# Masks of an attention stack between VectorE and GpSimd: ten steps of 32 in place of eleven, placed otherwise, and the output transposition ordered behind the mask of its own step

## The chip, the cores and the metric

The kernel runs on one core of one Trainium2 chip. The metric is the time of one execution on the device in microseconds (us), the median of several runs. Engines are named as the profile names them: PE is TensorE, DVE is VectorE, ACT is ScalarE, POOL is GpSimd, SP is the engine whose queue issues the DMAs. L557 is line 557 of the kernel.

## The reference

Sixteen sequences of 1024 tokens with 128 features go through three transformer layers with a shared adjacency mask and then through one graph attention layer. Cut to what matters:

```python
# layers 0 to 2 (8 heads of 16)
scores = einsum('bnhd,bmhd->bhnm', Q, K) / sqrt(16)
scores = where(adj == 0, -inf, scores)
attn_out = einsum('bhnm,bmhd->bnhd', softmax(scores), V)
x = layer_norm(x + attn_out @ Wo + bo)
x = layer_norm(x + relu(x @ W1 + b1) @ W2 + b2)
# layer 3: one head, scores s_i + s_j through a leaky relu, same mask, softmax, out + x, layer norm
```

## The kernel before, in words

**Passes and steps.** The work is cut into 48 passes. A pass is one sequence in one of the layers 0 to 2; four sequences go through the three layers side by side, so 12 passes make a round and there are four rounds. A pass has 32 steps: two groups of four heads, in each two halves of 512 queries, in each eight tiles of 128 keys. The line `order` in the main loop sets this sequence; n, held in `now[0]`, counts steps over the whole kernel.

**One step** (`score_step`, L537). Two score tiles of 128x1024 are made, each by two matmuls (L545) into a PSUM tile of the tag s, of which there are three (`slot`, L135). The first tile is called pp 0, the second pp 1. Each has to be masked and exponentiated, and there are two ways. On the POOL way ACT takes the exponential straight out of PSUM (L553) and POOL multiplies it by a mask of zeros and ones (L554). On the DVE way DVE adds a mask of zeros and large negative numbers while it reads PSUM (L557), and ACT takes the exponential in place (L569). pp 1 always goes the DVE way. pp 0 goes the POOL way, except in the steps that `BOTH_ON_DVE` (L41) names by their number within the pass, where both tiles go the DVE way. The PSUM tile is free again once L553 or L557 has read it.

**The sum over keys** (`av_step`, L571) follows four steps later (`AHEAD`, L40): eight matmuls (L574) add e times V into the one PSUM bank acc. After the eight key tiles of a half, at steps 3, 11, 19 and 27 of a pass, `finish` (L577) transposes acc on DVE (L585) into the tile tt, takes the reciprocals of the sums (L588, DVE) and lets POOL multiply (L589). The next half writes acc again from the following step on, so it has to wait for the transposition.

**Everything else** is a list of tasks, put into steps by the table `AT` (L34) and taken by `piece` (L871): projections of the next pass at steps 5 to 19 (`proj_tasks`, L457; ACT writes hi in L472 or L476, DVE writes the remainder lo in L473 or L477), the output projection of the pass before at 13 and 15, its first feed-forward matrix at 23 to 29 and its second at 31 and, of the pass before that, at 3. These matmuls (L383) use one PSUM bank, t. The sums and the norm's statistics are on DVE (L420, L413, L415), the norm itself on POOL (L433 to L435 and L441; all eight tiles at step 6 or so, four tiles each after steps 14 and 16), scale and shift on POOL (L511, L515, L632). DVE transposes x for the next layer and for the feed-forward (L357), and SP moves the result through memory (L361, L375). SP also copies hi and lo into the stacked form that the scores read (`stack`, L523). The graph attention of a finished sequence (`last_tasks`, L701) runs as further tasks during passes 10 to 14 of a round, in eight units of 128 queries (the loop of L826), with its edge masks on DVE (L774) and its norm and scaling on POOL (L798).

**What sets the order.** In the main loop PE, ACT and SP take their instructions in the order in which the program names them (`manual_schedule`, L957). DVE and POOL are ordered by a scheduler from priorities, before the kernel runs; on the chip they too run one instruction after the other in that order. Two tools correct the scheduler. `soon` (L333) raises the priority of an instruction by 120 places. `tc.issue_after(i)` puts an instruction behind instruction i on its engine. `behind["dve"]` holds the last mask addition that was named, `low` the lo instruction of each step that has one. L557 itself is put behind the lo of two steps earlier, where there is one.

Of the kernel before, what the change touches and what calls it, by code (L numbers as in the profile page):

```python
# [37 lines left out]
STACK_AT = 24  # L38
AT_END = {3: (12, 21, 22, 24, 25, 26, 27, 28, 30, 31), 2: (8, 9, 13, 14, 15, 16, 17, 18, 20, 21)}
AHEAD = 4  # L40
BOTH_ON_DVE = (2, 6, 7, 8, 17, 21, 23, 25, 26, 29, 30)  # L41
TILES = {"w": 8, "x": LANES + 1, "last": 2}
BLOCKED = -57344.0

# [75 lines left out]
def fast_path(ctx: ExitStack, tc: tile.TileContext, a: dict, out: bass.AP, flag):  # L120
# [24 lines left out]
    head, tail = [True], [False]  # L145
# [187 lines left out]
    def soon():  # L333

        return nullcontext() if head[0] else tc.high_priority(offset=SOON)
# [185 lines left out]
    behind, low = {}, {}  # L521
# [15 lines left out]
    def score_step(step):  # L537
# [3 lines left out]
        for pp in range(2):  # L541
# [6 lines left out]
            psv = ps.rearrange("p (r q) -> p r q", q=512)  # L548
            both = now[0] % (4 * NT) in BOTH_ON_DVE
            on_pool = pp == 0 and not both  # L550
# [26 lines left out]
    def finish(g, qh, acc):  # L577

        def run():
            if g == 0 and qh == 0:  # L580
                state["A"] = work.tile([P, 2, 16, G, HD], F32, tag="A", name="A", bufs=1)
                state["recs"] = work.tile([P, G, 2, 16], F32, tag="recs", name="recs", bufs=2)
            tt = work.tile([P, 16, SLOT], F32, tag="tt", name="tt", bufs=1)
            with soon(), tc.issue_after(low[now[0] - 2]) if now[0] - 2 in low else nullcontext():
                nc.vector.transpose(tt.rearrange("p a b -> p (a b)"), acc)  # L585
            rec = state["recs"][:, g, qh, :]
            with soon():
                nc.vector.reciprocal(rec, tt[:, :, HD])  # L588
                nc.gpsimd.tensor_mul(state["A"][:, qh, :, g, :], tt[:, :, :HD],  # L589
                                     rec[:, :, None].to_broadcast([P, 16, HD]))  # L590
        return run
# [246 lines left out]
    now = [0]  # L838
# [404 lines left out]
```

## Time and profile before

| what | value |
|---|---|
| median of 3 runs | 3936.28 us (3936.0 to 3938.77) |
| profiled execution, its own time | 3936.96 us |
| its span, first to last instruction | 3935.1 us |
| PE / DVE / ACT / POOL busy | 3742.7 / 3512.1 / 3289.2 / 3386.4 us |
| mask additions on DVE (L557) | 2064 of 1209 ns |
| mask multiplications on POOL (L554) | 1008 of 2026 ns |
| exponentials on ACT, from PSUM (L553) and in place (L569) | 1008 of 1024 ns, 2064 of 1061 ns |
| output transpositions on DVE (L585) | 192 of 706 ns |
| a pass without graph attention, such as the one from 469.65 to 540.58 us | 70.9 us |
| passes 10 to 15 of the first round (graph attention in them) | 74.0, 98.9, 91.3, 92.5, 95.3, 81.0 us |

How to read it: a busy time is a sum over the whole span, so a share says little about any one stage. PE's ends are modelled, so a busy PE is not PE at its peak. The start of a pass is the start of its first L545 matmul; the lengths of passes in the table are differences of such starts, and the start of each step follows by counting four L545 matmuls a step.

### The profile page before, as it was taken

The numbers are of one execution on the slowest core, as the hardware profiler recorded it, in microseconds if no ns is written. First come the engines' busy times: TensorE is split into PE (matmuls) and PEld (weight loads), VectorE is DVE, ScalarE is ACT, GpSimd is POOL, SyncE is SP. The second block draws the span as 40 slices with busy tenths as digits, with TensorE's granted clock in tenths as the row PEclk, the third lists the DMA queues.
The fourth block names the chain that finished last, engine by engine and source line by source line (L and its number), as shares of the span: only waits on it lengthen the run. The fifth ranks groups of instructions, "written<-read, shape, count | busy, mean of one in ns | idle before, by whom it ended". The sixth has DMA issues, their size and how long they took to land.

```text
span 3935.1 us, 109752 instructions
## 1 busy us (share of the span) xinstructions
PE 3742.7 (95%) x44385; PEld 1519.1 (39%) x44385; DVE 3512.1 (89%) x5908; ACT 3289.2 (84%) x3797; POOL 3386.4 (86%) x2923
## 2 busy tenths in 40 slices
PE   7999999999989999999998999999999999999987
PEld 2333333344434333334444433333444433333346
DVE  6999999989989999998998999998898999999876
ACT  7989999977877999997777899998776799999850
POOL 4889999978888999997888999998887899999784
PEclk8999999999999999999999999999999999999998
DMA  5423424322223423332322324333231324324200
GB/s 137 117 69 96 99 71 109 86 66 70 71 66 92 101 71 104 86 86 69 79 71 77 90 68 103 90 79 98 69 88 51 85 68 100 95 73 110 56 8 21
DMA packets 245889, 319.30 MB, mean 81 GB/s; under 512 B 51073, under 2 KB 174209, under 8 KB 245377
## 3 DMA queue, kind: packets, MB, share of 16 engines
q1 hardware_dynamic: 243840, 311.52, 31.3%
q8 instruction: 354, 5.80, 0.6%
q14 instruction: 159, 1.29, 0.1%
q10 hardware_dynamic: 1536, 0.68, 0.1%
HBM read 58.53 MB, written 51.38 MB: 28 GB/s over the span
## 4 chain that ended last, share of the span: by engine, by line
PE 50%; DVE 22%; ACT 11%; issue 6%; POOL 5%; DMA 3%; SPq 3%; DVEq 0%; ACTq 0%; POOLq 0%
PE acc L574 18%; DVE e L557 15%; PE t L383 15%; PE s L545 13%; ACT e L569 5%; ACT e L553 3%; POOL e L554 2%; PE s L769 2%; ACT hT L649 2%; PE s L383 1%; DMA x1T<-tr 1%; DVE st L413 1%; POOL x L441 1%; DVE xb L357 1%; DVE aT L603 1%
## 5 line engine op out<-in xcount | busy, mean ns | idle before, releaser
L557 DVE TENSOR_TENSOR e<-s,mask_add 128x1024 f32<-128x1024 f32 x2064 | 2417.5, 1209 | 136.7 <-PE s L545 99.2
L554 POOL TENSOR_TENSOR e<-e,mask 128x1024 f32<-128x1024 f32 x1008 | 2028.6, 2026 | 387.6 <-ACT e L553 373.8
L569 ACT ACTIVATE e<-e 128x1024 f32<-128x1024 f32 x2064 | 2144.6, 1061 | 176.9 <-DVE e L557 152.2
L574 PE MATMUL acc<-e,v 128*17 128x512 f32 x12288 | 1628.2, 602 | 12.7 <-POOL e L554 9.3
L545 PE MATMUL s<-Wq,Wk 64*128 64x512 f32 x6144 | 1228.6, 461 | 74.6 <-DVE e L557 32.0
L553 ACT ACTIVATE e<-s 128x1024 f32<-128x1024 f32 x1008 | 1031.9, 1024 | 294.1 <-PE s L545 279.5
L545 PEld LDWEIGHTS s<-Wq,Wk 64*128 64x128 f32 x6144 | 503.6, 185 | 1157.5 <-DVE e L557 464.3
L441 POOL TENSOR_SCALAR x<-x,mv 128x128 f32<-128x128 f32 x896 | 388.1, 448 | 19.5
L574 PEld LDWEIGHTS acc<-e,v 128*17 128x17 f32 x12288 | 205.7, 95 | 515.4 <-issue 428.3
L435 POOL TENSOR_TENSOR mv<-mv,half_neg 128x4 f32<-128x4 f32 (+1 forms) x179 | 213.9, 1195 | 14.1
L420 DVE TENSOR_TENSOR x<-t,x 128x512 f32<-128x512 f32 x191 | 131.9, 690 | 100.0 <-PE t L383 96.7
L413 DVE BATCH_NORM_STATS2 st<-x 128x6 f32<-128x128 f32 x896 | 204.6, 282 | 9.0
L774 DVE SCALAR_TENSOR_TENSOR ee<-s,mask 128x256 f32<-128x256 f32 x512 | 179.5, 412 | 32.4 <-PE s L769 32.4
L383 PE MATMUL t<-hd,ee 128*32 128x129 f32 x6656 | 205.7, 274 | 2.7 <-DVE x L420 2.7
L383 PE MATMUL t<-x1T,W 128*32 128x512 f32 x1520 | 199.3, 596 | 4.8 <-issue 2.4
L383 PEld LDWEIGHTS t<-W,hT 128*32 128x32 f32 x6080 | 169.2, 110 | 60.1 <-issue 48.7
L383 PEld LDWEIGHTS t<-hd,ee 128*32 128x32 f32 x6656 | 178.8, 109 | 16.4 <-DVE x L420 5.3
L383 PE MATMUL t<-W,hT 128*32 128x128 f32 x6080 | 183.6, 273 | 0.2
L585 DVE STREAM_TRANSPOSE tt<-acc 128x512 f32<-128x512 f32 x192 | 135.6, 706 | 33.4 <-PE acc L574 33.4
L649 ACT ACTIVATE hT<-t,b 128x512 f32<-128x512 f32 x190 | 130.6, 688 | 4.9 <-PE t L383 4.4
L515 POOL TENSOR_TENSOR x<-x,bo 128x1024 f32<-128x1024 f32 x48 | 114.6, 2388 | 9.2 <-DMA ai<-in_adj_dram 6.7
L589 POOL TENSOR_TENSOR A<-tt,recs 128x256 f32<-128x256 f32 x192 | 119.8, 624 | 0.2 <-DVE recs L588 0.2
(145 smaller groups left out, 2536.5 us busy)
## 6 DMA issues: line engine op xcount, KB each, us to landing
Wk<-hi SPq DMA_DIRECT2D x384, 128.0 KB
Wk<-lo SPq DMA_DIRECT2D x384, 128.0 KB
Wq<-hi SPq DMA_DIRECT2D x384, 128.0 KB
Wq<-lo SPq DMA_DIRECT2D x384, 128.0 KB
tr<-xb SPq DMA_DIRECT2D x656, 64.0 KB
x1T<-tr SPq DMA_DIRECT2D x90, 256.0 KB
xT<-tr SPq DMA_DIRECT2D x74, 256.0 KB
x<-in_x_dram SPq DMA_DIRECT2D x124, 64.0 KB
```

What stands on the lines that cost most here:

```text
L383: nc.tensor.matmul(dst[j:j + SLOT, :], cols, rhs, start=start, stop=stop)
L413: nc.vector.bn_stats(st[:, t, :], z[:, t, :])
L435: nc.gpsimd.tensor_tensor(v, v, half_neg[:, ts], OP.pow)
L441: nc.gpsimd.tensor_scalar(z[:, t, :], z[:, t, :], mv[:, t, 0:1], mv[:, t, 1:2], op0=OP.add, op1=OP.mult)
L545: nc.tensor.matmul(ps[:, r * 512:(r + 1) * 512], k[64 * r:64 * r + 64, kt * P:(kt + 1) * P], q[64 * r:64 * r + 64, q0:q0 + 512], start=Tru ...
L553: nc.scalar.activation(ev, psv, AF.Exp, scale=HD ** -0.5)
L554: behind["pool"] = nc.gpsimd.tensor_mul(ev, ev, m).ins
L557: behind["dve"] = nc.vector.tensor_add(ev, psv, m).ins
L569: nc.scalar.activation(ev, ev, AF.Exp, scale=HD ** -0.5)
L574: nc.tensor.matmul(acc[j * SLOT:j * SLOT + HD + 1, :], v_bufs[m % 2][:, kt, 2 * j + g, :], e[:, j, :], start=first, stop=last)
L649: nc.scalar.activation(s["h", f, h], ps, AF.Relu, bias=w["b1"][:, f:f + 1], scale=1.0)
L774: nc.vector.scalar_tensor_tensor(e[:, :, j * SLOT:(j + 1) * SLOT], ps.rearrange("p (k q) -> p k q", q=P)[:, :, j * SLOT:(j + 1) * SLOT], 1 ...
```

## The change

Two edits. The set of steps in which both tiles are masked on DVE has ten members in place of eleven, five of the ten are new places (3, 15, 24, 28, 31), and six old ones are gone (2, 6, 17, 21, 25, 29). And the transposition of acc (L585) is ordered behind the last mask addition that was named, which is that of its own step, in place of the lo of two steps earlier where there is one. The graph attention in eight units is in both kernels; the change does not touch it.

```diff
-BOTH_ON_DVE = (2, 6, 7, 8, 17, 21, 23, 25, 26, 29, 30)
+BOTH_ON_DVE = (3, 7, 8, 15, 23, 24, 26, 28, 30, 31)
...
             tt = work.tile([P, 16, SLOT], F32, tag="tt", name="tt", bufs=1)
-            with soon(), tc.issue_after(low[now[0] - 2]) if now[0] - 2 in low else nullcontext():
+            with soon(), tc.issue_after(behind["dve"]) if not tail[0] else nullcontext():
                 nc.vector.transpose(tt.rearrange("p a b -> p (a b)"), acc)
```

In the built programs PE's instructions stand in the same order before and after. On DVE and POOL the order differs. For a pass without graph attention, L557 and L554 written as the number of their step and the rest as their line, it is (STATS short for the statistics L413 and L415, NORM for L433 to L441):

```
DVE before   0 1 2 2 3 585 588 420 STATS 4 5 6 6 7 7 8 8 9 603 603 453 10 477 585 11 588 12 477 13 420 STATS
             14 15 420 STATS 16 17 17 357 477 18 19 585 588 20 477 21 21 357 22 23 23 24 357 25 25 26 26
             27 585 588 28 357 29 29 30 30 31 420 STATS
DVE after    0 1 2 3 3 585 588 420 STATS 4 5 6 7 7 8 8 9 603 603 453 10 477 11 585 588 12 477 13 420 STATS
             14 15 15 420 16 STATS 17 357 477 18 19 585 588 477 20 21 357 22 23 23 24 24 357 25 26 26
             27 585 588 28 28 357 29 30 30 31 31 420 STATS
POOL before  0 1 3 589 4 5 NORM8 9 10 11 589 12 13 14 NORM4 15 16 NORM4 18 19 589 20 22 632 24 632 27 589 28 511 515 31
POOL after   0 1 2 589 4 5 6 NORM8 9 10 11 589 12 13 14 NORM4 16 17 NORM4 18 19 589 20 21 22 632 632 25 27 589 511 29 515
```

## The prediction, made before the changed kernel ran

> **What bounds the kernel now.** I read the busy times first. No engine is idle enough to forget, so the question is who waits in a pass.
>
> ```profile
> PE 3742.7 (95%) x44385; PEld 1519.1 (39%) x44385; DVE 3512.1 (89%) x5908; ACT 3289.2 (84%) x3797; POOL 3386.4 (86%) x2923
> ```
>
> Then the busy times by stage, for one pass without graph attention (last line) and its parts: steps 0-3, 4-21, 22-28 and 29-31. Columns: stretch, its us, then busy us of PE, PEld, DVE, ACT, POOL.
>
> ```profile
> 469.65:478.32 8.67, 8.64 (x116) 3.67 (x112) 8.35 (x16) 7.71 (x8) 6.79 (x4) 1.00 0.64 161
> 478.32:517.48 39.16, 37.81 (x380) 12.97 (x376) 36.55 (x62) 36.48 (x41) 36.02 (x39) 1.00 0.17 42
> 517.48:532.59 15.11, 14.94 (x113) 4.12 (x109) 14.83 (x16) 14.89 (x18) 15.09 (x9) 1.00 0.49 123
> 532.59:540.58 7.99, 7.82 (x112) 3.49 (x108) 6.73 (x7) 7.78 (x9) 7.91 (x6) 1.00 0.70 162
> 469.65:540.58 70.93, 69.21 (x708) 24.25 (x704) 66.46 (x99) 66.86 (x74) 65.81 (x55) 1.00 0.36 87
> ```
>
> DVE, ACT and POOL all have 66 of 70.9 us, and POOL is already full from step 22 to the end. For PE I count from the timeline: an unhindered step (scores and sum) starts the next after 1.64 us; other matmuls add 0.86 or 0.87 in twelve steps and 1.75 in two. 32 x 1.64 + 12 x 0.865 + 2 x 1.75 = 66.4. So PE loses 4.5 us a pass. Where, PE's timeline shows: always ahead of the second score tile of a step, which needs a PSUM tile back.
>
> ```profile
> 492.85 0.50 PE L545 MATMUL s<-Wq,Wk 64*128 64x512 f32 x2
> 493.76 0.50 PE L545 MATMUL s<-Wq,Wk 64*128 64x512 f32 x2 [0.41 <-DVE e L557]
> ...
> 511.78 0.50 PE L545 MATMUL s<-Wq,Wk 64*128 64x512 f32 x2 [0.60 <-ACT e L553]
> ```
>
> By step the loss is 0.31 (step 3), 0.37 (9), 0.68 (11), 0.53 (13), 0.87 (19) and 1.6 together in 21, 22, 23, 25 and 29. At 9, 11 and 13 it is DVE that is late. DVE's timeline says why at 11: it stands idle at the transposition L585, which waits for PE's last sum, while the mask of step 11 queues behind it.
>
> ```profile
> 492.49 1.21 DVE L557 TENSOR_TENSOR e<-s,mask_add 128x1024 f32<-128x1024 f32 x1
> 493.62 0.74 DVE L477 SCALAR_TENSOR_TENSOR lo<-t,bqkv,hi 128x512 fp32r<-128x512 f32 x1
> 495.31 0.72 DVE L585 STREAM_TRANSPOSE tt<-acc 128x512 f32<-128x512 f32 x1 [0.95 <-PE acc L574]
> 495.95 1.18 DVE L557 TENSOR_TENSOR e<-s,mask_add 128x1024 f32<-128x1024 f32 x1
> ```
>
> POOL's timeline shows its only idle time in the pass: 1.80 ahead of the mask of step 3, 0.25 (step 4), 1.05 (9), 0.41 (10), 0.39 (14), each for an exponential of ACT.
>
> ```profile
> 477.19 2.03 POOL L554 TENSOR_TENSOR e<-e,mask 128x1024 f32<-128x1024 f32 x1 [1.80 <-ACT e L553]
> 491.08 2.02 POOL L554 TENSOR_TENSOR e<-e,mask 128x1024 f32<-128x1024 f32 x1 [1.05 <-ACT e L553]
> 493.51 4.01 POOL L554 TENSOR_TENSOR e<-e,mask 128x1024 f32<-128x1024 f32 x2 [0.41 <-ACT e L553]
> 502.45 2.03 POOL L554 TENSOR_TENSOR e<-e,mask 128x1024 f32<-128x1024 f32 x1 [0.39 <-ACT e L553]
> ```
>
> **What the Trainium skill says.** "Perfetto Trace Analysis", Identifying the Most-Contended Engine: a busy share measures Vector, Scalar and GpSimd fairly, PE's matmul share does not; hence my own count for PE (69.2 busy, 66.4 needed). The same page, Optimization Strategy, takes a gap that repeats as a sign of too few buffers; the gap ahead of the second score tile is one, with three s tiles. "PSUM — Partial Sum Buffer", Engine vs sequencer instructions: the queues of ScalarE, VectorE and GpSimdE are strictly first in, first out; the 0.95 us of L585 with a mask behind it agree. "GPSIMD Engine Reference", 3.1 Elementwise, has a two-input add take 1.96 times as long on GpSimd as on VectorE; here it is 2026 to 1209 ns, 1.68, and I use those.
>
> **The change part by part.** Sums are against the profiled execution, 3936.96 us (span 3935.1), 0.7 above the median of 3936.28.
>
> *Eleven to ten.* 48 masks leave DVE and go to POOL, one a pass. DVE loses 1.21 us a pass (66.46 to 65.25); POOL gains 2.03 (65.81 to 67.84); ACT has one L553 of 1024 ns for one L569 of 1061 ns, nothing. POOL becomes the fullest engine, and 67.8 a floor. DVE's relief pays only where DVE is last; POOL's load costs nothing only if it falls into POOL's idle 3.9 us.
>
> *Where it falls on POOL.* From the order: between the masks of steps 14 and 4 of the next pass POOL had 13 multiplications and the 1.80 us of idle time; now it has 14 and no wait for step 3. The idle time takes the 2.0 us. Between steps 4 and 13 it had eight (3, 4, 5, 9-13; 3 is replaced by 6) and still has eight, so the norms at 14 and 16 start as before. The order around 18 to 20 is the same too, 16 and 17 standing where 15 and 16 stood.
>
> *Steps 3 and 9 to 13 (PE).* Without the second mask of step 6 everything on DVE from there is 1.13 us earlier (the distance of two masks in the timeline): the wait of 0.37 at 9 goes, that at 11 shrinks to some 0.3. With L585 behind mask 11, that mask needs not wait for PE's sum: it starts at once, some 1.7 us earlier, so mask 12 and the wait at 13 (0.53) go. Step 3's wait halves, since ACT, not DVE, now frees that tile. Together 1.4 us.
>
> *Steps 15 to 22.* The mask of 17 (pp 0) is exchanged for that of 15, that of 21 for one of 24: DVE is where it was at 17 and ahead from 21. ACT gets to step 18 some 0.3 earlier; 0.4 of the 0.87 at step 19 goes. Steps 21 to 23 wait for ACT as before.
>
> *Steps 24 to 31.* The waits at 25 and 29 (0.28 + 0.44) go, as DVE is 1.1 ahead. That makes 2.5 us a pass for PE alone.
>
> *What is late next: POOL.* Follow it from the mask of step 4, for which it must wait for ACT (1.65 after the step's start, as now). Up to the mask of 18 there are 12 multiplications at 1.98 (start to start), eight norm tiles 5.86, two times four 6.94, one L589 0.58: 37.2, with 0.2 for the wait at 6. The sum over step 18 is due 0.7 into step 22. So steps 4 to 21 take at least 1.65 + 37.4 - 0.7 = 38.35, against 39.16. Steps 22 to 28: 19, 20, 21, 22, 25, one L589, two L632 of 2.36 make 15.2; now 15.11, so nothing is won. Steps 29 to 3: PE needs 15.9, and now takes 16.66. In all 69.45, a gain of 1.4 to 1.5 a pass, 1.4 taken.
>
> *The transposition alone.* At 3, 19 and 27 L585 already stood behind its step's mask; only step 11 changes. The wait that it adds: L585 and L588 stand behind a mask of 1.2 us, and PE's next sum (step 12) behind L585. Mask 11 ends as PE's last sum ends, so L585 ends some 0.3 before PE wants acc; without that cover it costs up to 0.9 a pass.
>
> *DMA.* No transfer is added. The copies that feed the next pass's scores are issued up to 534.94 and wanted at 540.58, and start from the L357 of step 22, which is not later.
>
> *Graph attention passes.* There PE is nearly never kept waiting (90.8 of 91.26 us busy in pass 12), so little is to be had: passes 12 to 14 -0.5 each; pass 11 +1, since POOL has one mask more ahead of step 27, whose sum had 0.9 us to spare. Pass 15 is the bad one: there POOL is behind, its masks of 15, 18, 19 and 20 end just as PE needs them, and one more (step 17) ahead of 18 costs up to 2.0, taken as 1.5. Passes 10, 22, 34, 46: -0.5 each.
>
> *Sum.* 25 plain passes (3-9, 16-21, 28-33, 40-45) x -1.4 = -35; passes 1 and 2 -2; the four -2; three rounds of passes 11-15 with (1 - 1.5 + 1.5) +3; pass 0 and the end after pass 46 nothing, as chains of DMA and PE set them (bounds -2 and +4). -36: 3901 in the profile's terms, 3900 as a median.
>
> **The rivals.** (a) *POOL does not pace* (0.20): what I count as POOL's chain has slack, and PE's 2.5 us come through: 25 x -2.5 and -5 elsewhere, 3868. For: ACT may come earlier as well. Against: POOL is full from step 22. (b) *No change* (0.14): the waits move from DVE to ACT and POOL, and a pass stays at 70.9; 3936, at most 8 either way. For: ACT's waits at 19 to 23 stay. (c) *Slower, through POOL* (0.20): POOL's idle 3.9 us stay because they wait for ACT, not for work. Then a pass needs 67.84 and what is left of them; from 3.1 us on it is slower than 70.93. With all 3.9 and 0.6 lost in turning from one engine to the other it is 72.3, 25 x 1.4 and three times 2 in pass 15: 3977. It shows as PE waiting at the sums of 18 to 25. Against: the idle time ahead of step 3 goes by the order alone. That the eight units do something is no case: they are in both kernels.
>
> **How the numbers follow.** The likeliest (0.46) is 3900, its own range 3884 to 3918. With (a) down to 3856 and (b) up to 3944 this holds 0.8; since (c) is open above, I take 3858 to 3956. About 0.2%, 8 us, is what can be told from no change. Faster by more: 0.46 + 0.20 + 0.02 = 0.68; within: 0.12; slower: 0.20.
>
> **What would show it.** Plain passes of 69 to 70 us; POOL at 98% in them; no wait of L585 for PE at step 11 beyond 0.3; PE's waits at 9 and 13 gone, new short ones at the sums of 18 to 25 for POOL. It is wrong if PE's waits for PSUM tiles in 19 to 29 grow, since then ACT or DVE is late by the new places; or if pass 15 grows by over 2 us.

## The result, and the profile after

| | before | changed |
|---|---|---|
| median | 3937.25 us (7 runs, 3936.0 to 3940.11) | 3922.55 us (7 runs, 3921.27 to 3926.47) |
| ratio | | 0.9963, 95% interval 0.9952 to 0.9975 |
| profiled execution, its span | 3936.96, 3935.1 us | 3922.55, 3920.7 us |
| median plain pass | 70.93 us | 70.41 us |

The changed kernel is 14.7 us faster, where 36 were forecast. First the busy times of the changed kernel, and then the head of the chain that ended last, by engine: before, then after.

```profile
PE 3715.7 (95%) x44385; PEld 1515.1 (39%) x44385; DVE 3460.5 (88%) x5860; ACT 3296.9 (84%) x3797; POOL 3477.6 (89%) x2971
```

```profile
PE 50%; DVE 22%; ACT 11%; issue 6%; POOL 5%; DMA 3%; SPq 3%; DVEq 0%; ACTq 0%; POOLq 0%
```

```profile
POOL 46%; PE 38%; ACT 5%; DVE 5%; issue 3%; SPq 2%; DMA 1%; DVEq 0%; ACTq 0%; POOLq 0%
```

POOL's busy share rises by three points only, but its share of the chain goes from 5% to 46%: it has become what the kernel waits for. The same plain pass as before, cut at the same steps (0-3, 4-21, 22-28, 29-31, then the whole; busy us of PE, PEld, DVE, ACT, POOL), in the changed kernel:

```profile
462.72:471.30 8.58, 8.58 (x118) 3.68 (x114) 8.37 (x16) 7.71 (x9) 8.22 (x4) 1.00 0.76 190
471.30:509.34 38.04, 37.57 (x380) 12.94 (x376) 35.48 (x62) 36.27 (x41) 35.72 (x39) 1.00 0.14 35
509.34:525.07 15.73, 14.61 (x112) 4.02 (x108) 13.99 (x15) 15.19 (x18) 15.65 (x9) 1.00 0.63 146
525.07:533.10 8.03, 7.76 (x112) 3.49 (x108) 7.57 (x8) 7.87 (x9) 8.03 (x6) 1.00 0.60 142
462.72:533.10 70.38, 68.52 (x708) 24.13 (x704) 65.41 (x99) 67.03 (x75) 67.63 (x56) 1.00 0.38 91
```

Steps 4 to 21 are 1.1 us shorter, steps 22 to 28 are 0.6 longer. What is late there is seen at PE's sums of the steps 18, 19, 21 and 25 (PE's timeline, changed kernel):

```profile
510.88 1.05 PE L574 MATMUL acc<-e,v 128*17 128x512 f32 x8 [0.60 <-POOL e L554]
512.85 1.05 PE L574 MATMUL acc<-e,v 128*17 128x512 f32 x8 [0.26 <-POOL e L554]
...
517.40 1.05 PE L574 MATMUL acc<-e,v 128*17 128x512 f32 x8 [0.27 <-POOL e L554]
...
526.19 1.05 PE L574 MATMUL acc<-e,v 128*17 128x512 f32 x8 [0.27 <-POOL e L554]
```

Each waits for a multiplication of POOL. Before, the sums of 18 and 25 had no such wait (PE, before; the pass of the prediction):

```profile
518.39 1.05 PE L574 MATMUL acc<-e,v 128*17 128x512 f32 x8
...
533.69 1.05 PE L574 MATMUL acc<-e,v 128*17 128x512 f32 x8
```

And all of POOL's idle time that the profile marks in the pass, from POOL's timeline; it was 3.9 us and is 1.6:

```profile
471.66 0.62 POOL L589 TENSOR_TENSOR A<-tt,recs 128x256 f32<-128x256 f32 x1 [0.72 <-DVE recs L588]
473.00 4.01 POOL L554 TENSOR_TENSOR e<-e,mask 128x1024 f32<-128x1024 f32 x2 [0.72 <-ACT e L553]
477.20 2.03 POOL L554 TENSOR_TENSOR e<-e,mask 128x1024 f32<-128x1024 f32 x1 [0.19 <-ACT e L553]
```

The idle time lies at steps 3, 4 and 6. From 477.20 to the end of the pass the profile marks none. At step 11 (PE, then DVE) the transposition no longer waits, but PE still does:

```profile
486.35 0.50 PE L545 MATMUL s<-Wq,Wk 64*128 64x512 f32 x2 [0.42 <-DVE e L557]
```

```profile
486.96 1.23 DVE L557 TENSOR_TENSOR e<-s,mask_add 128x1024 f32<-128x1024 f32 x1
488.10 0.70 DVE L585 STREAM_TRANSPOSE tt<-acc 128x512 f32<-128x512 f32 x1
```

By groups of passes, the profiled execution against that of before, in us (a minus is a gain): plain passes -12.9 (25 times -0.5); passes 0 to 2 -5.2; 10, 22, 34, 46 +3.8; 11, 23, 35 -9.5; the kinds 12 and 13 -2.6; 14, 26, 38 +7.8; 15, 27, 39 +9.0; from pass 47 on -4.6.

### The profile page after: what moved, and what is told of

Its sections match the earlier page's. It is cut to its first block, busy times and chain, and to the rows that moved or that the text cites. A ratio compares the mean times of both kernels' runs of the same rounds, so it can differ in the third digit from the quotient of the medians.

```text
span 3920.7 us, 109674 instructions
## 1 busy us (share of the span) xinstructions
PE 3715.7 (95%) x44385; PEld 1515.1 (39%) x44385; DVE 3460.5 (88%) x5860; ACT 3296.9 (84%) x3797; POOL 3477.6 (89%) x2971
## 4 chain that ended last, share of the span: by engine, by line
POOL 46%; PE 38%; ACT 5%; DVE 5%; issue 3%; SPq 2%; DMA 1%; DVEq 0%; ACTq 0%; POOLq 0%
POOL e L554 27%; PE acc L574 13%; PE t L383 12%; PE s L545 9%; POOL x L441 7%; POOL mv L435 4%; POOL x L632 4%; ACT e L553 3%; DVE e L557 3%; ACT e L569 2%; PE s L769 2%; POOL x L798 2%; PE s L383 1%; POOL A L589 1%; SPq L530 1%
## 5 line engine op out<-in xcount | busy, mean ns | idle before, releaser
L557 DVE TENSOR_TENSOR e<-s,mask_add 128x1024 f32<-128x1024 f32 x2016 | 2377.4, 1211 | 240.3 <-PE s L545 214.5
L554 POOL TENSOR_TENSOR e<-e,mask 128x1024 f32<-128x1024 f32 x1056 | 2120.1, 2029 | 241.6 <-ACT e L553 227.8
L569 ACT ACTIVATE e<-e 128x1024 f32<-128x1024 f32 x2016 | 2110.9, 1062 | 185.2 <-DVE e L557 156.3
L553 ACT ACTIVATE e<-s 128x1024 f32<-128x1024 f32 x1056 | 1083.3, 1026 | 250.6 <-PE s L545 244.8
L545 PE MATMUL s<-Wq,Wk 64*128 64x512 f32 x6144 | 1196.4, 458 | 32.3 <-DVE e L557 21.1
L441 POOL TENSOR_SCALAR x<-x,mv 128x128 f32<-128x128 f32 x896 | 388.1, 448 | 19.1
L413 DVE BATCH_NORM_STATS2 st<-x 128x6 f32<-128x128 f32 x896 | 204.0, 281 | 7.7
L585 DVE STREAM_TRANSPOSE tt<-acc 128x512 f32<-128x512 f32 x192 | 135.3, 705 | 0.0
L357 DVE STREAM_TRANSPOSE xb<-x 128x512 f32<-128x512 f32 x164 | 115.0, 701 | 20.1 <-POOL x L441 19.9
```

The source lines that it names most:

```text
L413: nc.vector.bn_stats(st[:, t, :], z[:, t, :])
L441: nc.gpsimd.tensor_scalar(z[:, t, :], z[:, t, :], mv[:, t, 0:1], mv[:, t, 1:2], op0=OP.add, op1=OP.mult)
L545: nc.tensor.matmul(ps[:, r * 512:(r + 1) * 512], k[64 * r:64 * r + 64, kt * P:(kt + 1) * P], q[64 * r:64 * r + 64, q0:q0 + 512], start=Tru ...
L553: nc.scalar.activation(ev, psv, AF.Exp, scale=HD ** -0.5)
L554: behind["pool"] = nc.gpsimd.tensor_mul(ev, ev, m).ins
L557: behind["dve"] = nc.vector.tensor_add(ev, psv, m).ins
```

## The experiments

The theory so far: in a plain pass (one without graph attention) POOL's queue, from the mask of step 4 to that of step 25, sets the time. The letters of theories and rivals below are those of the expectations, which were written before each run. The rivals: VectorE and its PSUM tiles pace and POOL only follows; POOL's total counts and not the place; the gain is the transposition's. Lines of a diff are against the changed kernel unless said otherwise. Ratios are to the kernel before on the same chip, with 95% intervals; "14+15" is the growth of the six passes 14, 15, 26, 27, 38, 39 together, and a plain pass is the median of 25.

| run | median us | ratio | plain pass us | 14+15 us |
|---|---|---|---|---|
| transposition alone | 3932.99 | 0.9983 (0.9977 to 0.9990) | 70.59 | +1.0 |
| set alone | 3930.75 | 0.9981 (0.9973 to 0.9989) | 70.51 | +18.4 |
| mask 20 back | 3916.99 | 0.9945 (0.9932 to 0.9959) | 69.79 | +18.9 |
| x1T behind mask 19 | 3937.13 | 0.9994 (0.9986 to 1.0002) | 70.50 | +17.9 |
| mask 6 back | 3906.39 | 0.9922 (0.9908 to 0.9935) | 69.85 | +3.0 |
| old steps near last | 3904.74 | 0.9913 (0.9900 to 0.9927) | 69.71 | +3.4 |
| nine steps | 4014.06 | 1.0195 (1.0181 to 1.0209) | 72.64 | +29.7 |
| step 2 for 3 | 3931.29 | 0.9981 (0.9973 to 0.9988) | 70.52 | +17.3 |
| 6 near last | 3905.07 | 0.9910 (0.9895 to 0.9925) | 69.79 | +2.5 |
| masks 6 and 20 back | 3898.39 | 0.9894 (0.9879 to 0.9909) | 69.38 | +5.1 |
| without L515 | 3921.44 | 0.9953 (0.9939 to 0.9966) | 70.50 | +10.3 |
| without the add of L632 | 3916.05 | 0.9937 (0.9923 to 0.9950) | 70.14 | +17.6 |
| changed kernel again | 3924.36 | 0.9965 (0.9951 to 0.9979) | 70.45 | +16.7 |
| before again | 3938.82 | 1.0006 (0.9997 to 1.0014) | 70.92 | +0.2 |
| steps by pass | 3891.03 | 0.9878 (0.9861 to 0.9894) | 69.38 | 0.0 |

### The two edits apart

The transposition alone (against before), and the set alone (against the changed kernel):

```diff
-            with soon(), tc.issue_after(low[now[0] - 2]) if now[0] - 2 in low else nullcontext():
+            with soon(), tc.issue_after(behind["dve"]) if not tail[0] else nullcontext():
```

> The old eleven steps with the transposition ordered behind its step's mask; what is computed is unchanged. Theory A (GpSimd's queue paces the changed kernel, the transposition is a small part): only step 11 changes, the 0.95 us for which VectorE stood at L585 with mask 11 behind it go, and with GpSimd still idle 3.9 us a pass some of that comes through: a plain pass 70.6 instead of 70.9, the kernel 3927 to 3933. Theory B (the gain of the changed kernel is the transposition's, the ten steps give nothing): the whole gain is here, 3921 to 3926. Theory C (the wait at step 11 is covered): 3935 to 3939.

```diff
-            with soon(), tc.issue_after(behind["dve"]) if not tail[0] else nullcontext():
+            with soon(), tc.issue_after(low[now[0] - 2]) if now[0] - 2 in low else nullcontext():
```

> The new ten steps with the old order of the transposition; what is computed is unchanged. Theory A: GpSimd paces from step 4 to step 25, so what VectorE loses again at step 11 is hidden: plain passes 70.4 to 70.5, the kernel 3921 to 3926, as with both edits. Theory B (the gain is the transposition's): 3934 to 3939.

Measured: 70.59 and 70.51 us a plain pass, against 70.93 with neither and 70.41 with both. Theory A held for the transposition alone, theories B and C fell; the set alone came out near 3931, between A and B, though its plain passes are A's. The two gains do not add. The median steps of the plain passes show why: the transposition shortens step 13 by 0.34 us with either set (3.04 to 2.70), but with the new set step 22, where PE waits for POOL, grows from 2.26 to 2.53. Most of what DVE wins at 13, POOL takes back at 22. The growth of passes 14 and 15 is the set's alone.

### One mask more or less on POOL

Step 20, or step 6, added to the set; step 15 taken out; both added:

```diff
-BOTH_ON_DVE = (3, 7, 8, 15, 23, 24, 26, 28, 30, 31)
+BOTH_ON_DVE = (3, 7, 8, 15, 20, 23, 24, 26, 28, 30, 31)
```

> The changed kernel with an eleventh step, 20: one mask of 2.0 us leaves GpSimd just where its masks end as the sums of 18 to 25 need them, and VectorE has one of 1.2 us more. What is computed is unchanged. Theory A (GpSimd's queue paces): the waits of TensorE for GpSimd at the sums of 20, 21 and 25 go; the plain pass falls from 70.4 to 69.4 to 69.8 (then the scores' PSUM tiles are next), the kernel to 3897 to 3910; passes 14 and 15, in which GpSimd is late too, do not grow further. Theory D (VectorE and ScalarE pace, GpSimd's lateness at the sums only follows them): VectorE's 1.2 us more make it slower, plain passes 70.9 or more, the kernel 3935 to 3950.

```diff
-BOTH_ON_DVE = (3, 7, 8, 15, 23, 24, 26, 28, 30, 31)
+BOTH_ON_DVE = (3, 6, 7, 8, 15, 23, 24, 26, 28, 30, 31)
```

> The changed kernel with an eleventh step, 6, which takes one mask of 2.0 us off GpSimd ahead of its norm of eight tiles. What is computed is unchanged. Theory F (in passes 14 and 15 GpSimd is late by just that mask): their growth of 16.7 us over the three rounds goes, both types within 1 us a pass of before. In a plain pass the chain of GpSimd from mask 4 to the sum of 18 ends 2.0 us earlier, so TensorE's 0.6 in step 22 go, and VectorE's waits at 9 and 17 come back in part: 69.8 to 70.2 us; the kernel 3893 to 3908. Theory H (passes 14 and 15 grow by the new places from 15 on, not by 6): they stay at +2.5 or more each, the kernel 3908 to 3918.

```diff
-BOTH_ON_DVE = (3, 7, 8, 15, 23, 24, 26, 28, 30, 31)
+BOTH_ON_DVE = (3, 7, 8, 23, 24, 26, 28, 30, 31)
```

> The changed kernel with nine steps: 15 is masked on GpSimd, 2.0 us more between its two norms of four tiles, and VectorE has 1.2 us less. What is computed is unchanged. Theory A (GpSimd's queue from mask 4 to the sum of 25 sets a plain pass): the whole 2.0 us show, plain passes 72.3 to 72.5, the kernel 3970 to 3985 with the passes 14 and 15. Theory D (VectorE and ScalarE pace and GpSimd follows): 70.0 to 70.6 and 3905 to 3925. Between the two, 71 to 71.5, if GpSimd has slack of half a mask there.

```diff
-BOTH_ON_DVE = (3, 7, 8, 15, 23, 24, 26, 28, 30, 31)
+BOTH_ON_DVE = (3, 6, 7, 8, 15, 20, 23, 24, 26, 28, 30, 31)
```

> Twelve steps: 6 and 20 both on VectorE, in all passes. GpSimd has 4.0 us less before the sum of 25 than in the changed kernel, VectorE 2.4 us more a pass, 67.7 of some 69.7. What is computed is unchanged. Theory A (beyond the first mask given back GpSimd no longer sets the pass, VectorE and its PSUM tiles do): the second mask gives little or takes, plain passes 69.5 to 70.2, so no more than 0.3 better than with either alone; passes 14 and 15 as with 6 back, pass 14 up to 1 longer; 3900 to 3915. Rival L (GpSimd still paces with either mask back): the second mask brings another 0.6, plain passes 69.1 to 69.3, the kernel 3886 to 3894.

With 20 back, a plain pass is 69.79; theory D wanted 70.9 or more and fell. The kernel's 3917 missed A's range, since passes 14 and 15 stayed long and 14 grew. With 6 back it is 69.85, and the growth of 14 and 15 falls from 16.7 to 3.0 us: theory F held. Of the 2.0 us taken off POOL only 0.56 come through in a plain pass: POOL now waits for exponentials again, 1.07 us at the mask of 9 and 0.40 at that of 10, and step 9 is back at 2.86 us. With 20 back the sums of 18 and 19 still wait for POOL, as mask 20 comes after them (PE, mask 20 back):

```profile
509.63 1.05 PE L574 MATMUL acc<-e,v 128*17 128x512 f32 x8 [0.60 <-POOL e L554]
511.61 1.05 PE L574 MATMUL acc<-e,v 128*17 128x512 f32 x8 [0.26 <-POOL e L554]
514.12 1.05 PE L574 MATMUL acc<-e,v 128*17 128x512 f32 x8
```

With both back those waits are gone, and the second mask brings 0.4 more. That was expected of neither: A had 69.5 or more, L 69.3 or less. What holds PE now is VectorE: the only waits of PE that the profile marks in the pass are 0.42 us at step 11 and 0.30 at step 22, both for an L557. The chain and POOL's idle time agree (masks 6 and 20 back: chain by engine; then the pass's busy times; then POOL's longest two waits):

```profile
PE 56%; DVE 25%; POOL 7%; issue 5%; ACT 3%; SPq 2%; DMA 1%; DVEq 0%; ACTq 0%; POOLq 0%
```

```profile
463.31:532.68 69.37, 68.51 (x708) 24.29 (x704) 67.18 (x101) 66.50 (x75) 63.91 (x54) 1.00 0.36 89
```

```profile
472.25 0.62 POOL L589 TENSOR_TENSOR A<-tt,recs 128x256 f32<-128x256 f32 x1 [1.22 <-DVE recs L588]
...
484.66 2.03 POOL L554 TENSOR_TENSOR e<-e,mask 128x1024 f32<-128x1024 f32 x1 [1.05 <-ACT e L553]
```

POOL is back at 7% of the chain; VectorE has 25%.

Nine steps came out at 72.64 in most passes, at 73.65 to 74.04 in eight of the 25, and at 4014 for the kernel; A had 72.3 to 72.5 and up to 3985. The order shows who waits: mask 17 now stands behind the second norm of four tiles, not ahead of it (POOL, then PE at the sum of 17, nine steps):

```profile
512.74 4.00 POOL L554 TENSOR_TENSOR e<-e,mask 128x1024 f32<-128x1024 f32 x2
516.83 0.24 POOL L433 TENSOR_SCALAR mv<-mv 128x4 f32<-128x4 f32 x1
...
518.60 1.75 POOL L441 TENSOR_SCALAR x<-x,mv 128x128 f32<-128x128 f32 x4
520.31 5.95 POOL L554 TENSOR_TENSOR e<-e,mask 128x1024 f32<-128x1024 f32 x3
```

```profile
522.38 1.33 PE L574 MATMUL acc<-e,v 128*17 128x512 f32 x8 [3.04 <-POOL e L554]
```

The sum takes 1.33 us there, not 1.05: the granted clock of PE is lower. In the same columns as above (the clock is the number behind POOL's), passes 5, 6 and 16 of nine steps:

```profile
400.26:474.13 73.87, 70.45 (x708) 24.43 (x704) 64.78 (x98) 66.59 (x75) 70.62 (x57) 0.95 0.34 87
474.13:546.78 72.65, 69.19 (x708) 24.19 (x704) 64.83 (x98) 66.39 (x75) 68.83 (x57) 0.98 0.33 88
1309.39:1381.84 72.45, 67.94 (x708) 23.95 (x705) 64.78 (x98) 67.07 (x75) 69.74 (x57) 1.00 0.37 93
```

The clock stands at a half for 6.8 us about the wait at the sum of 17 in exactly the eight long passes, for 3.4 us in 16 others, and nowhere in pass 16, which took 72.45 (70.69 in the changed kernel). No other run has such a stretch in a plain pass. So in the one pass at the full clock the mask on POOL cost 1.8 us, near the 2.0 that A forecast, and the eight long passes have 1.0 to 1.4 us more that go with the clock. That the clock makes this difference was not tested by a run.

### The same work of POOL, at two places

One addition of 2.4 us is left out, once behind step 29 and once ahead of mask 25; then step 2 for 3, which moves POOL's wait:

```diff
         def shift():
-            with tc.issue_after(behind["pool"]) if m else nullcontext():
+            if not m:
                 nc.gpsimd.tensor_add(x, x, rows(W[l]["bo"]))
```

> The changed kernel without the addition of L515 from pass 1 on (the bias of the output projection is left out of the result), 2.4 us of GpSimd a pass behind step 29. Theory A (GpSimd is held by TensorE again at mask 4; what it does between mask 27 and mask 4 has 1.4 us of slack, work before the sum of 25 has none): plain passes 70.2 to 70.4, the kernel 3912 to 3924. Rival M (GpSimd's total of 68.7 us a pass is what counts): 2.4 us less show for a large part, plain passes 69.0 to 69.8, the kernel 3885 to 3908.

```diff
         def x1_by(op, v):
             def run():
+                if v == "b2":
+                    return
                 with tc.issue_after(behind["pool"]):
```

> The changed kernel without the second addition of L632 (the bias of the feed-forward is left out of the result), the same 2.4 us of GpSimd a pass, but just ahead of the mask of step 25. Theory A: the wait of TensorE at the sum of 25 goes, and with it 0.3 to 0.6 us a pass, until the masks of 18 to 20 alone hold it: plain passes 69.8 to 70.1, the kernel 3903 to 3913. Rival M (the total counts, the place does not): the same time as without L515.

```diff
-BOTH_ON_DVE = (3, 7, 8, 15, 23, 24, 26, 28, 30, 31)
+BOTH_ON_DVE = (2, 7, 8, 15, 23, 24, 26, 28, 30, 31)
```

> The changed kernel with step 2 in place of step 3, so that GpSimd waits for the exponential of step 3 as it did before, with ten steps. What is computed is unchanged. Theory A (GpSimd is held by TensorE again at mask 4, so its wait ahead of mask 3 lies in slack, and only the stretch from mask 4 to the sum of 25 counts): plain passes 70.3 to 70.6, the kernel 3917 to 3928. Theory K (the prediction's step, that the idle 1.8 us ahead of mask 3 has to go for the added mask to be free): the idle time comes back and is paid, plain passes 71.2 or more, the kernel 3940 to 3960.

Without L515 a plain pass is 70.50, no gain: POOL waits 1.78 us more at the next pass's first mask (POOL, without L515).

```profile
464.88 6.01 POOL L554 TENSOR_TENSOR e<-e,mask 128x1024 f32<-128x1024 f32 x3 [1.78 <-ACT e L553]
```

Without the addition of L632 it is 70.14, so 0.3 better; the wait at the sum of 25 goes, those at 18, 19 and 21 stay (PE):

```profile
508.27 1.05 PE L574 MATMUL acc<-e,v 128*17 128x512 f32 x8 [0.66 <-POOL e L554]
...
523.25 1.05 PE L574 MATMUL acc<-e,v 128*17 128x512 f32 x8
```

The kernel's 3916 is above A's 3903 to 3913, but rival M, for which both are alike, falls on the plain passes: 70.50 and 70.14. Step 2 for 3 has POOL waiting 1.22 us ahead of mask 3 again, and a plain pass is 70.52, 0.1 from the changed kernel: K falls. The kernel's 3931 lies above A's 3928 all the same; in the profiled execution most of what it has over the changed kernel lies in passes 11, 23 and 35 and from pass 47 on. POOL is anchored at mask 4, for which it waits in any case; between mask 27 and mask 4 it has 1.4 us to spare, between 4 and 25 only the 0.19 at mask 6.

### Passes 14 and 15

```diff
-AT = {"xP": (4, 6), "proj": (5, 7, 9, 11, 17, 19), "post": (13, 15, 17, 18, 21, 22, 22, 23, 24, 25, 27, 29, 31, 35, 38, 40)}
+AT = {"xP": (4, 6), "proj": (5, 7, 9, 11, 17, 19), "post": (13, 15, 19, 20, 21, 22, 22, 23, 24, 25, 27, 29, 31, 35, 38, 40)}
...
-    def moved(dst, src):
+    def moved(dst, src, gap=3):
...
-        return [(2, send(0), "*"), (1, get(0), "*"), (3, send(1), "*"), (1, get(1), "*")]
+        return [(2, send(0), "*"), (1, get(0), "*"), (gap, send(1), "*"), (1, get(1), "*")]
...
-            together += moved(x1T, x1)
+            together += moved(x1T, x1, 1)
```

> The changed kernel with one instruction a pass moved: the first L357 transposition of the feed-forward's input stands behind mask 19 and L585 on VectorE in place of behind mask 17. What is computed is unchanged. Theory E (in passes 14 and 15 GpSimd's norm is late, L357 waits for it, and the masks of 18 and 19 behind L357 hold TensorE): the growth of passes 14 and 15 (2.8 and 2.7, 2.8 and 3.5, 2.2 and 2.8 us in the three rounds, 16.7 in all) goes for its larger part, pass 2 and the plain passes stay, the kernel 3905 to 3912. Theory F (GpSimd itself is late there, and its masks of 18 to 20 hold the sums): passes 14 and 15 stay long, 3918 to 3925. If moving it makes the feed-forward late, its first matrix at step 23 waits for the transfer and plain passes grow: over 3925.

In pass 14 of the changed kernel DVE stands at L357 and has the masks of 18 and 19 behind it:

```profile
1154.70 0.71 DVE L357 STREAM_TRANSPOSE xb<-x 128x512 f32<-128x512 f32 x1 [3.21 <-POOL x L441]
...
1155.91 2.34 DVE L557 TENSOR_TENSOR e<-s,mask_add 128x1024 f32<-128x1024 f32 x2
```

With L357 moved, these masks come 3.5 us earlier after their scores (1.08 in place of 4.58 us), yet the six passes stay at +17.9: theory E fell. PE merely waits for POOL at the sum of 18 instead, 2.73 us in pass 14. So the wait at L357 was POOL's lateness, seen on another engine. (The kernel itself came to 3937, level with before and 12 us above F's range. Its profiled execution, at 3931.9 the fastest of 13, has plain passes of 70.50, and most of what it has over the changed kernel lies in passes 11, 23 and 35 and from pass 47 on; why the other executions are longer still is open.)

Where the lateness comes from, POOL's timeline of pass 14 shows, at the mask of step 6 and the norm of eight tiles:

```profile
1123.80 2.03 POOL L554 TENSOR_TENSOR e<-e,mask 128x1024 f32<-128x1024 f32 x1 [1.16 <-DMA Wk<-hi]
1125.91 0.25 POOL L433 TENSOR_SCALAR mv<-mv 128x8 f32<-128x8 f32 x1
1126.23 0.25 POOL L434 TENSOR_SCALAR mv<-mv 128x8 f32<-128x8 f32 x1
1126.45 2.40 POOL L515 TENSOR_TENSOR x<-x,bo 128x1024 f32<-128x1024 f32 x1
1128.80 1.67 POOL L435 TENSOR_TENSOR mv<-mv,half_neg 128x8 f32<-128x8 f32 x1
1130.43 2.39 POOL L798 TENSOR_TENSOR x<-x,ln_g 128x1024 f32<-128x1024 f32 x1
```

The first line is the mask of step 6, which was VectorE's before; behind it 10.3 us of norm, scaling and shift follow without a break, and then the masks from 9 on. With 6 back on VectorE the growth is 3.0; without L515, which lies in this stretch in pass 14, the three passes 14 grow by 1.2 in place of 7.8, and the three passes 15, where L515 does not, still by 9.1. A lower clock is not what makes it: pass 39 of the changed kernel grew by 2.8 with the full clock throughout.

### The set by pass

The old set, or the new with 6, in the passes with graph attention and eleven steps with 20 elsewhere; then twelve steps but in passes 12 to 14. In the second run the line of BOTH_NEAR_LAST is `(3, 6, 7, 8, 15, 23, 24, 26, 28, 30, 31)`:

```diff
-BOTH_ON_DVE = (3, 7, 8, 15, 23, 24, 26, 28, 30, 31)
+BOTH_ON_DVE = (3, 7, 8, 15, 20, 23, 24, 26, 28, 30, 31)
+BOTH_NEAR_LAST = (2, 6, 7, 8, 17, 21, 23, 25, 26, 29, 30)
...
-            both = now[0] % (4 * NT) in BOTH_ON_DVE
+            both = now[0] % (4 * NT) in (BOTH_NEAR_LAST if step[0] >= 10 and (step[0] - 10) % 12 < 6 else BOTH_ON_DVE)
```

> The eleven steps with 20 in the plain passes and the old eleven steps in the six passes of each round that have graph attention in them or carry its tail (10 to 15, 22 to 27, 34 to 39, 46 and 47), both with the transposition behind its mask. What is computed is unchanged. If the passes are independent of one another, each keeps the time it had with its set: -28.8 us for the 25 plain passes and -4.6 for 0 to 2 (as with mask 20 back), 0 to +2 for the graph attention passes and -1 for the end (as with the transposition alone): 3902 to 3908, faster than before and after. If what the plain passes win is taken back by the DMA chain of the graph attention, passes 10 and 11 grow by several us: 3912 to 3920.

> The eleven steps with 20 in the plain passes, and the ten new steps plus 6 in the passes with graph attention (10 to 15, 22 to 27, 34 to 39, 46, 47). What is computed is unchanged. If each pass keeps the time that it had with its set: -28 to -31 us for the plain passes, -5 for 0 to 2, and for the graph attention passes -0.5 in all (as with mask 6 back everywhere) and -2 at the end: 3898 to 3903, the fastest so far. If passes 10 and 11 depend on when the passes before them end rather than on their set: 3903 to 3910.

```diff
-BOTH_ON_DVE = (3, 7, 8, 15, 23, 24, 26, 28, 30, 31)
+BOTH_ON_DVE = (3, 6, 7, 8, 15, 20, 23, 24, 26, 28, 30, 31)
+WITHOUT = {0: (6, 20), 1: (6, 20), 2: (20,)}
...
-            both = now[0] % (4 * NT) in BOTH_ON_DVE
+            at = now[0] % (4 * NT)
+            both = at in BOTH_ON_DVE and not (step[0] >= 12 and at in WITHOUT.get(step[0] % 12, ()))
```

> Twelve steps (with 6 and 20) in all passes but 12 and 13 of a round, which have the ten of the changed kernel, and 14, which has eleven (6 without 20). What is computed is unchanged. If each pass keeps what it had with its set: 10.5 us below twelve steps everywhere, 3886 to 3892, the fastest. If what is won in 12 to 14 is lost in 15, which starts with GpSimd later: 3893 to 3900.

By groups of passes all three keep roughly what each pass had with its set, within 2.4 us a group but for two groups of the second run: passes 11, 23 and 35 (2.6) and pass 47 on (4.4). The kernels take 3904.7, 3905.1 and 3891.0 us. The second lies 2 us above the range for passes that keep their time, and within that for passes 10 and 11 that do not; by the groups more of it comes from pass 47 on than from these. The third is the fastest of all, 1.2% below before.

### The same two kernels again

No edit: the changed kernel and the kernel before, once more.

> The changed kernel once more, unaltered. If the -9.5 us in passes 11, 23 and 35 and the -4.6 at the end belong to the change, they come again within 1 us each. If they hang on when transfers land in an execution, the three passes 11 come to -2 to -5 and the end to -1.5 to -3, while plain passes stay at 70.4 and passes 14 and 15 at +2 to +3.5 each. The kernel 3921 to 3930.

> The kernel before once more, unaltered. Plain passes 70.9. If executions differ in passes 10, 11 and the end, these differ from the first profile by several us; if not, by less than 1. The kernel 3935 to 3941.

The kernel before repeats itself within 0.4 us in every group but passes 0 to 2 (+0.5). The changed kernel repeats its plain passes within 0.1 and the sum 14+15, which is split otherwise (6.8 and 10.0 in place of 7.8 and 9.0), but passes 11, 23 and 35 come to -6.4 in place of -9.5, and from pass 47 on -2.3 in place of -4.6. About 3 and 2 us of the first profile's gain there belong to that execution.

For passes 11, 23 and 35 the traces show what differs. In step 0 PE waits for a DMA (into h_rows or g_rows), and the clock of PE may stand at a half for some us after it. The first 12 us of passes 11 and 23 in the first profile of the changed kernel, then of 23 and 35 in the second:

```profile
821.12:833.12 12.00, 11.79 (x196) 6.53 (x192) 11.04 (x26) 7.92 (x8) 6.07 (x3) 1.00 0.50 138
1777.72:1789.72 12.00, 9.99 (x122) 4.58 (x118) 8.28 (x21) 6.99 (x8) 6.04 (x3) 0.86 0.48 125
```

```profile
1779.74:1791.74 12.00, 10.58 (x156) 5.55 (x156) 10.18 (x26) 7.18 (x9) 6.02 (x3) 1.00 0.54 130
2738.92:2750.92 12.00, 8.93 (x92) 3.93 (x92) 7.76 (x20) 6.70 (x8) 5.53 (x3) 0.86 0.43 119
```

Where the clock is 1.00 the pass gained 4.8 and 3.2 us; where it is 0.86 it gained 0.9 and lost 0.2. In all 17 traces there are 51 such passes. Against the first profile of the kernel before, those without a half-clock stretch in their first 9 us are 2.8 to 4.8 us shorter, those with one of 3.4 us lie between 2.2 shorter and 0.3 longer, and those with a longer one, as all six of the kernel before, between 0.8 shorter and 1.9 longer. How much of this is the wait and how much the clock was not separated, nor why the DMA lands when it does.

## Why the prediction was right in kind and wrong in size

**What holds.** The direction, the engine and the form: POOL becomes the bound, PE waits at the sums of 18 to 25 for it, L585 does not wait at 11, the waits at 9 and most of 13 are gone. POOL was busy for 96% of a plain pass (67.6 of 70.4 us), not 98. Rival (a), that POOL does not pace, fell with masks 6 and 20 back and with nine steps; (b) by the interval; (c), POOL's idle time stays, since 2.3 of the 3.9 us went.

**The step that failed: "In all 69.45".** A plain pass takes 70.39. Cut as the sum was (the sum of 18 starts at 510.88 and that of 25 at 526.19, both due 0.7 into their step; step 4 starts at 471.30, and at 541.69 in the next pass):

| term | forecast | measured |
|---|---|---|
| steps 4 to 21, POOL | 38.35 | 38.88 |
| 22 to 28, POOL | 15.2 | 15.31 |
| 29 to 3, PE | 15.9 | 16.20 |

The first term's 0.5: twelve multiplications were taken at 1.98 us, their distance in a row. The timeline has 24.3 us for them, not 23.8, as one ahead of a norm takes 2.1 to the next start and the last counts to its end and the start of the sum. The third term's 0.3: PE was given what it needs, though step 3 keeps 0.2 of its wait of 0.31; it was to halve, and went from 3.70 to 3.61 us. Each is at most 2% of its term; together, 0.94, they are two thirds of the gain forecast, which was the difference of two times of 70 us. 25 times 0.9 is about 22 us, by which the plain passes miss their forecast of -35; the whole forecast is off by 21.

**"Eleven to ten".** The idle 3.9 us were to take the mask. As it stands, the mask is not free: with 6 left on VectorE a plain pass is 0.56 shorter and the kernel 16 us faster (3906.4 to 3922.6, on two chips; 0.9922 to 0.9963). Of the ladder nine, ten, eleven, twelve steps (72.64, 70.41, 69.8, 69.38 us a plain pass) the change went one rung the wrong way in the plain passes; its gain there is that of the new places and of the transposition. The sum saw that POOL would be full and stopped there; it never set a step more against a step less. (The first rung holds the lower clock too.)

**"Where it falls on POOL".** The count there is not that of the order which stands ahead of the prediction. Between mask 14 and mask 4 of the next pass there are 13 multiplications in both kernels, step 2 in place of step 3; the prediction has 14 after the change. Its eight between 4 and 13 take in the mask of 3, which stands ahead of 4; without it they were seven and are now eight. So the added mask is that of step 6, behind mask 4. Not the 1.80 us ahead of mask 3 took it, but the waits of 1.05, 0.41 and 0.39 us at 9, 10 and 14, which are gone. That the wait ahead of mask 3 is worth nothing, step 2 for 3 shows: 1.22 us of it come back, and a plain pass stays at 70.52. The 69.45 does not hang on this count, since its chain has the mask of 6 in it.

**"Steps 3 and 9 to 13", "15 to 22", "24 to 31".** The wait at 9 went as forecast (step 9 from 2.86 to 2.51 us). At 11 it stays (3.18, 3.19). At 19, 0.71 went, not 0.4, but 17 lost 0.33. Those at 25 and 29 were to go and did, but the steps are no shorter (2.78 to 2.84, 2.94 to 2.96 us): the sums of 21 and 25, which PE does in these steps, now wait for POOL. With both masks back the steps do fall, to 2.54 and 2.61.

**"The transposition alone".** The paragraph asks only what it costs, and finds it covered. By itself it gains 0.34 a plain pass with the old set, and 0.10 with the new.

**"Graph attention passes".** Forecast -1 in all outside the plain passes, measured -1.3, by errors that cancel; that this sum fits is luck. Pass 15 was the right suspect, and its growth of 2.7 to 3.5 us is over the 2 us that the prediction had named as a sign that it is wrong; but the mask that hurts most is 6, ahead of the eight-tile norm, not 17: +9.0 in place of +4.5. In pass 14, put down at -1.5 without following POOL, it is +7.8. Passes 10, 22, 34 and 46 were put at -2 and took +3.8: in pass 10 mask 25 stands behind two L632 and one L798 (PE, changed kernel).

```profile
812.68 1.05 PE L574 MATMUL acc<-e,v 128*17 128x512 f32 x8 [2.50 <-POOL e L554]
```

In pass 10 and in pass 34 a half-clock stretch of 3.4 us goes with this wait, and they took 2.5 and 2.6 us more; pass 22 has none and took 1.0.

Passes 11, 23 and 35, put at +1 each, gained 9.5 together. The DMA for which pass 11 waits in step 0 (4.05 us before) is issued from pass 10 on, so what 10 loses lies partly in that wait; 10 and 11 together are -2.3, +0.1 and -1.2 in the three rounds.

## What to carry to other kernels

When all engines are nearly full, count the chain of the engine that becomes the bound from start to start as the timeline has it, handovers and last ends included, and give the gain the error of that whole chain, not of the difference. Work that moves to such an engine is free only between two points where it waits anyway: find where its queue is anchored (here mask 4) and by when it is due (here the sum of 25), and look at each kind of pass for what would stand behind the work that is added. A wait that appears on another engine's queue can be the same lateness a second time: taking the wait away did nothing here, taking the mask away did. And read the granted clock of a pass before a longer pass is put down to its queue alone.

## What the runs showed of the hardware

It seems that POOL can hold DVE without a wait that the profile names. In pass 2 DVE scales weights (L304) while POOL multiplies masks: the first line is one such instruction with POOL free, the second one that began while POOL's two masks of the last line ran (before; DVE, DVE, POOL):

```profile
208.10 0.28 DVE L304 TENSOR_SCALAR Wq<-Wq,ln_gc 128x128 f32<-128x128 f32 x1
...
219.05 2.02 DVE L304 TENSOR_SCALAR Wq<-Wq,ln_gc 128x128 f32<-128x128 f32 x1
```

```profile
216.95 4.04 POOL L554 TENSOR_TENSOR e<-e,mask 128x1024 f32<-128x1024 f32 x2
```

0.28 us become 2.02, and it ends at 221.07, 0.08 us after POOL's second mask. The Trainium skill's "SBUF — State Buffer", SBUF: two separate sides, describes a port pair that GpSimd and some instructions of VectorE share as an exclusive lock, held for a whole instruction; these two durations agree, though no run here isolates it. The two masks of step 17 stood behind this on DVE before, one mask of it after. That may be a part of the 4.3 us which pass 2 gained; it was not measured by itself, and a half-clock stretch in pass 2 is also shorter, 3.4 us in place of 6.8.

The granted clock of PE was seen at a half in stretches of 3.4 us or a multiple of it (but for one at an execution's end), and of like waits one was followed by such a stretch and the other not: with nine steps the sum of 17 waited 2.99, 3.04 and 3.02 us in passes 5, 6 and 16, and the half clock then lasted 6.8 us, 3.4 us and not at all. At the half clock a sum of eight matmuls took up to 1.91 us, not 1.05.
